# q, k and v by Strassen's scheme in a two-layer attention kernel, with shared activation sums and an earlier bias of q

## The chip, the cores and the metric

The kernel runs on one NeuronCore of a Trainium2 chip. The metric is the device time of one execution in microseconds (us), as a median over runs. Engines are called as in the profile: PE is TensorE (matmuls), PEld its weight loads, DVE is VectorE, ACT is ScalarE, POOL is GpSimd, SP is SyncE, which only starts DMAs here.

## The reference, cut to what matters

Two attention layers are computed on `x` of 8 images x 512 channels x 32 x 32 positions (1024 tokens), all in float32. Only the first layer's opening is touched by the change:

```python
h = group_norm(xf, gn_w, gn_b)                       # 8 x 512 x 1024
qkv = jnp.einsum('oc,bct->bot', qkv_w, h) + qkv_b[None, :, None]
q, k, v = jnp.split(qkv, 3, axis=1)                  # 8 heads of 64 channels
q = fake_quant(q)                                    # scale from min and max of the whole tensor
k = fake_quant(k)
v = fake_quant(v)
```

After it come softmax attention per head, a projection with the residual, and the second layer (norm, one-head attention over 512 channels, projection, residual). Because `fake_quant` takes its scale from the minimum and maximum over all images, q, k and v of all images have to be there before the first attention score.

## The kernel before, in words

The work has two stages. Stage 1 computes q, k and v of all images, stores them in DRAM and gathers their extremes. Stage 2 first turns the extremes into scales and then runs attention, projection and the whole second layer, with the matmuls of several images woven into one another by a planner (`attention`, `fold`, `others`, lines 438 to 756). `mm` (line 93) ties every matmul to the one before it, so TensorE runs them exactly in the order in which the program makes them; one matmul that waits holds all that follow. The other engines' queues are static too; their order is laid down when the program is built, and an instruction that needs nothing may be put ahead of one that stands earlier in the text.

In stage 1 an image `b` (0 to 7) has its 512 channels on 128 partitions as 4 chunks `cc`, and its 1024 tokens as two halves `hf` of 512. `load_x` (line 231) loads it on SP's queue. `norm_steps` (line 100) is a generator: statistics of each chunk and half on VectorE (lines 107 and 108), a small matmul with `gavg` that averages over the channels of a group (line 111), four small VectorE operations, a second small matmul (line 121), the power on GpSimd (line 124), and 8 scalings into `h` (line 128). The loop calls it as `ahead` for image b+1 while image b is multiplied, one step at a time.

q and k of an image are 8 tiles `t` of 128 channels (0 to 3 are q, 4 to 7 are k; `j` is t modulo 4). Each takes 8 matmuls of 512 columns into a pair of PSUM banks (`pair_ps`, two pairs in all). VectorE then adds the bias, writes the tile to SBUF and takes the maximum in one instruction (line 321), takes the minimum in a second (line 325), and SP stores the tile (line 326). v of an image is 8 tiles of 128 tokens, each of 4 matmuls into one bank (`bank`, two in all), then an add of the bias, a maximum, a minimum and a store (lines 343 to 346).

Image 0 is opened by hand: its norm is cut into the 4 chunks, and the matmuls of its first two tiles (`early`) go chunk by chunk as the norm gets ready. `bias` (line 264) multiplies the weights with the norm's shift: 4 matmuls of 512 columns, then for q and k `by_channel` (line 213: four multiplications by the identity, line 216, and a reduction, line 217) and an add. For q it stands after the opening's last matmul. The weights that stage 2 folds into one another (`wn`: NQ1 and NK1 in tile `h`, NV1 and WP1 in tile `v`) are loaded on SP's queue at b = 1. The pool `l1p` has one buffer for each tag (`h`, `v`, `g`, `rs`, `rs1`, `acc1`), which stage 2 uses too.

At the end of stage 1, lines 351 to 374 reduce the extremes over all partitions, VectorE quantises the first pair, and TensorE meanwhile runs the first half of `fold` (line 674): 16 matmuls on `wn_h` before the first scores, then 16 on `wn_v` between the next scores.

Of the kernel before, what the change touches and what calls it, by code (L numbers as in the profile page):

```python
# [9 lines left out]
F32 = mybir.dt.float32  # L10
# [36 lines left out]
def attn_pair_kernel(  # L47
# [51 lines left out]

    def norm_steps(src, dst, wcol, bank, nm, ccs=range(CC)):  # L100

# [3 lines left out]
        for i, cc in enumerate(ccs):  # L105
            for hf in range(NH):
                nc.vector.bn_stats(st[:, i, hf, :], src(cc, hf))
            nc.vector.bn_aggr(mv[:, i, :], st[:, i, :, :].rearrange("p a s -> p (a s)"))
        yield
        ps = bank(f"gps_{nm}")[:, 0:n]  # L110
# [15 lines left out]
        for hf in range(NH):  # L126
            for i, cc in enumerate(ccs):
# [3 lines left out]
                )  # L131
        yield

# [19 lines left out]
    with ExitStack() as fast:  # L153
# [5 lines left out]
        def pair_ps(name):  # L159
            return ps_s.tile([P, 2, 512], F32, tag="s", name=name)  # L160
# [4 lines left out]
        def bank(name):  # L165
            return ps_o.tile([P, 512], F32, tag="o", name=name)
# [11 lines left out]

        qmax = wts.tile([P, B * PAIRS], F32, name="qmax")
        qmin = wts.tile([P, B * PAIRS], F32, name="qmin")  # L180
        kmax = wts.tile([P, B * PAIRS], F32, name="kmax")
        kmin = wts.tile([P, B * PAIRS], F32, name="kmin")
        vmax = wts.tile([P, B * NT], F32, name="vmax")
        vmin = wts.tile([P, B * NT], F32, name="vmin")

# [4 lines left out]
        NR0, NR1 = B * PAIRS * 16, B * NH * 4  # L190
        rcs = l1p.tile([P, NR0 + NR1], F32, name="rcs")
        rs_d = [dram.tile([4, 512], F32, tag=f"rs{n}", name=f"rs_d{n}") for n in range(B * PAIRS)]
        rs1_d = [dram.tile([4, P], F32, tag=f"rs1{n}", name=f"rs1_d{n}") for n in range(B * NH)]
# [24 lines left out]

        with tc.tile_pool(name="p1w", bufs=1) as p1w, tc.tile_pool(name="p1", bufs=2) as p1, tc.tile_pool(
            name="p1o", bufs=4  # L220
        ) as p1o:
            wqkv = p1w.tile([P, CC, 3 * C], F32, name="wqkv")

            wn = {}
            for tag, ij in (("h", (NQ1, NK1)), ("v", (NV1, WP1))):
                two = l1p.tile([P, 2, CC, C], F32, tag=tag, name=f"wn_{tag}")
                for n, i in enumerate(ij):
                    wn[i] = two[:, n]
            xs, hs = {}, {}

# [6 lines left out]

            def norm(b, parts=1):

                xt = xs.pop(b)  # L240
                hs[b] = hn = p1.tile([P, CC, T], F32, tag="h", name=f"h1_{b}")
                n = CC // parts
                return [
                    norm_steps(
                        lambda cc, hf: xt[:, cc, bass.ts(hf, 512)],
                        lambda cc, hf: hn[:, cc, bass.ts(hf, 512)],
                        V_GN0W, av_bank, f"a{b}_{i}", range(i * n, (i + 1) * n),
                    )
                    for i in range(parts)
                ]  # L250

            load_x(0)
            for i in (1, 2):
                nc.sync.dma_start(
                    wqkv[:, :, bass.ts(i, C)], w_qkv[:, :, bass.ts(i, C)]
                )
            vb = p1w.tile([P, C], F32, name="vb")
            nc.scalar.dma_start(vb, vbias[0:1, :].partition_broadcast(P))
            load_x(1)
            gbb = p1w.tile([P, CC, P], F32, name="gbb")  # L260
            widen(gbb, V_GN0B)
            qkb = p1w.tile([P, 2 * PAIRS], F32, name="qkb")

            def bias(i):

                ps = bank(f"bias{i}")
                for _ in weigh(ps, ((wqkv[:, :, bass.ts(i, C)], gbb),)):
                    pass
                if i == 2:
                    nc.vector.tensor_add(vb, vb, ps)  # L270
                    return
                b4 = qkb[:, bass.ts(i, PAIRS)]
                by_channel(b4, ps)
                nc.vector.tensor_add(
                    b4, b4, vec[:, V_QKB + i * PAIRS : V_QKB + (i + 1) * PAIRS]
                )
# [14 lines left out]
            for cc in range(CC):  # L291
                for t in range(2):
                    for hf in range(NH):
                        qk_mm(0, early[t], t, hf, cc)
                        if (cc, hf) in ((0, 1), (1, 0), (1, 1)):
                            next(next(then, iter(())), None)
            for b in range(B):
                ahead = norm(b + 1)[0] if b + 1 < B else iter(())
                next(ahead, None)
                if b + 2 < B:  # L300
                    load_x(b + 2)
                if b == 1:
                    nc.sync.dma_start(wp0, w_sq[WP0])
                    for i, w in wn.items():
                        nc.sync.dma_start(w, w_sq[i])
                hn = hs[b]
                for t in range(2 * PAIRS):
                    isk, j = divmod(t, PAIRS)
                    g = b * PAIRS + j
                    if b == 0 and t < 2:  # L310
                        ps = early[t]
                    else:
                        ps = pair_ps(f"qkps_{b}_{t}")
                        for hf in range(NH):
                            for cc in range(CC):
                                qk_mm(b, ps, t, hf, cc)
                    if b == 0 and j == 0:
                        bias(isk)
                    qk = p1o.tile([P, T], F32, tag="qk", name=f"qk1_{b}_{t}")
                    mx, mn = (kmax, kmin) if isk else (qmax, qmin)  # L320
                    nc.vector.tensor_scalar(  # L321
                        qk, ps.rearrange("p a n -> p (a n)"), qkb[:, t : t + 1], None,
                        ALU.add, ALU.max, accum_out=mx[:, g : g + 1],
                    )
                    nc.vector.tensor_reduce(mn[:, g : g + 1], qk, AX.X, ALU.min)
                    nc.sync.dma_start((k_d if isk else q_d)[b][j], qk)
                    if t in (3, 5, 6):
                        next(ahead, None)
                for t in range(NT):
                    g = b * NT + t  # L330
                    ps = bank(f"vps_{b}_{t}")
                    for cc in range(CC):
                        mm(
                            ps,
                            lhsT=hn[:, cc, bass.ts(t, P)],
                            rhs=wqkv[:, cc, 2 * C : 3 * C],
                            start=(cc == 0),
                            stop=(cc == CC - 1),
                        )
                    if b == 0 and t == 0:  # L340
                        bias(2)
                    vt = p1o.tile([P, C], F32, tag="v", name=f"v1_{b}_{t}")
                    nc.vector.tensor_add(vt, ps, vb)
                    nc.vector.tensor_reduce(vmax[:, g : g + 1], vt, AX.X, ALU.max)
                    nc.vector.tensor_reduce(vmin[:, g : g + 1], vt, AX.X, ALU.min)
                    nc.sync.dma_start(v_d[b][:, t, :], vt)
                del hs[b]

# [769 lines left out]
```

## Time and profile before

| what | value |
|---|---|
| median of 3 runs | 2965.43 us (2964.5 to 2966.43) |
| the profiled execution's own time | 2966.03 us |
| its span, first to last instruction | 2964.5 us |
| mean granted clock of TensorE | 0.998 of full |
| TensorE busy | 2932.2 us, 8772 instructions |
| VectorE busy | 1442.7 us |
| ScalarE busy | 718.6 us |
| first q and k matmul of image 0 starts | 14.0 us |
| last matmul of stage 1 ends | 700.57 us |

A row of a group reads: line, engine, operation, tile written, tiles read, shapes, count, then the busy time in us and the mean of one in ns, then the idle time of the engine just before and what ended it. In the chain, pieces stand in order of time with start and length. `x` counts instructions. All matmuls stand under line 94, the helper `mm`, so the tile's name tells which they are: `qkps` is q and k, `vps` is v, `gps_a` the norm's small ones. Rows on one engine may overlap by some tens of ns.

### The profile page before, as it was taken

The numbers are of one execution on the slowest core, as the hardware profiler recorded it, in microseconds if no ns is written. First come the engines' busy times: TensorE is split into PE (matmuls) and PEld (weight loads), VectorE is DVE, ScalarE is ACT, GpSimd is POOL, SyncE is SP. The second block draws the span as 40 slices with busy tenths as digits, with TensorE's granted clock in tenths as the row PEclk, the third lists the DMA queues.
The fourth block names the chain that finished last, engine by engine and source line by source line (L and its number), as shares of the span: only waits on it lengthen the run. The fifth ranks groups of instructions, "written<-read, shape, count | busy, mean of one in ns | idle before, by whom it ended". The sixth has DMA issues, their size and how long they took to land.

```text
span 2964.5 us, 22733 instructions
## 1 busy us (share of the span) xinstructions
PE 2932.2 (99%) x8772; PEld 1170.9 (39%) x8772; DVE 1442.7 (49%) x1980; ACT 718.6 (24%) x825; POOL 26.1 (1%) x28
## 2 busy tenths in 40 slices
PE   7999999999999999999999999999999999999999
PEld 3444444443233333333333333334333333333443
DVE  5555554446874446345544544463446444543311
ACT  0000000002642333233233233332333332332001
POOL 0000000000000000000000000000000000000000
PEclk9999999999999999999999999999999999999999
DMA  6322221123220111012011211110211021000000
GB/s 244 114 107 102 107 107 75 71 78 128 79 65 29 61 50 54 15 61 73 31 44 48 67 36 58 40 54 29 61 54 50 23 67 61 15 26 29 18 14 23
DMA packets 112518, 182.81 MB, mean 62 GB/s; under 512 B 22032, under 2 KB 54800, under 8 KB 111760
## 3 DMA queue, kind: packets, MB, share of 16 engines
q1 hardware_dynamic: 112112, 180.98, 18.1%
q8 instruction: 70, 1.15, 0.2%
q10 hardware_dynamic: 288, 0.29, 0.1%
q14 instruction: 48, 0.39, 0.0%
HBM read 113.53 MB, written 67.40 MB: 61 GB/s over the span
## 4 chain that ended last, share of the span: by engine, by line
PE 95%; DVE 2%; DMA 1%; issue 1%; SPq 0%; POOL 0%; ACT 0%; DVEq 0%; POOLq 0%; ACTq 0%
PE o L94 15%; PE s L94 15%; PE qkps L94 15%; PE av L94 14%; PE g L94 8%; PE v2ps L94 7%; PE pj L94 7%; PE vps L94 7%; PE st L94 4%; DVE acc L464 1%; PE sm L94 1%; PE fold L94 1%; DMA rs<-rs_d 0%; PE bias L94 0%; DMA raw<-k_d 0%
## 5 line engine op out<-in xcount | busy, mean ns | idle before, releaser
L459 ACT ACTIVATE pt<-st,esc 128x1024 f32<-128x1024 f32 x512 | 542.3, 1112 | 665.6 <-PE st L94 664.2
L464 DVE TENSOR_TENSOR acc<-acc,pt 128x1024 f32<-128x1024 f32 x384 | 469.9, 1224 | 208.1 <-ACT pt L459 192.6
L94 PE MATMUL av<-pt,v 128*64 128x512 f32 x2048 | 476.6, 601 | 0.0
L94 PE MATMUL qkps<-h,wqkv 128*128 128x512 f32 x1024 | 449.5, 598 | 8.8 <-DVE qk L321 6.6
L94 PE MATMUL o<-p,v 128*128 128x512 f32 x1024 | 452.1, 596 | 1.5 <-DVE x L663 1.5
L94 PE MATMUL s<-g,h 128*128 128x512 f32 x1024 | 450.3, 596 | 0.0
L94 PEld LDWEIGHTS qkps<-h,wqkv 128*128 128x128 f32 x1024 | 194.3, 192 | 246.4 <-issue 240.9
L94 PEld LDWEIGHTS s<-g,h 128*128 128x128 f32 x1024 | 191.7, 190 | 243.4 <-issue 242.6
L94 PEld LDWEIGHTS o<-p,v 128*128 128x128 f32 x1024 | 191.5, 190 | 241.6 <-issue 240.0
L94 PEld LDWEIGHTS av<-pt,v 128*64 128x64 f32 x2048 | 132.2, 136 | 260.9 <-issue 260.9
L94 PE MATMUL pj<-ao,wp 128*128 128x512 f32 x512 | 226.0, 597 | 2.4 <-DVE ao L501 2.4
L94 PE MATMUL g<-h,wa 128*128 128x512 f32 x512 | 224.9, 595 | 0.0
L94 PE MATMUL v2ps<-wm,h 128*128 128x512 f32 x512 | 222.9, 594 | 0.0
L94 PE MATMUL vps<-wqkv,h 128*128 128x512 f32 x512 | 221.3, 592 | 0.8 <-DVE vb L270 0.8
L321 DVE TENSOR_SCALAR_CACHE_REDUCE qk<-qkps,qkb 128x1024 f32<-128x1024 f32 x64 | 82.1, 1283 | 222.7 <-PE qkps L94 222.6
L685 ACT COPY wa<-fold 128x512 f32<-128x512 f32 x4 | 2.3, 586 | 709.2 <-PE fold L94 709.2
L631 ACT ACTIVATE p<-s 128x512 f32<-128x512 f32 x128 | 76.4, 597 | 364.0 <-PE s L94 364.0
L635 DVE TENSOR_TENSOR acc<-acc,p 128x512 f32<-128x512 f32 x96 | 66.4, 692 | 186.4 <-ACT p L631 186.4
L94 PE MATMUL st<-q,k 64*128 64x512 bf16 x1024 | 156.5, 382 | 0.0
L462 DVE TENSOR_TENSOR acc<-pt,pt 128x1024 f32<-128x1024 f32 x64 | 78.3, 1224 | 140.0 <-ACT pt L459 140.0
L94 PEld LDWEIGHTS vps<-wqkv,h 128*128 128x128 f32 x512 | 97.2, 190 | 123.6 <-issue 122.0
L94 PEld LDWEIGHTS pj<-ao,wp 128*128 128x128 f32 x512 | 96.0, 190 | 124.8 <-issue 119.4
(118 smaller groups left out, 1315.1 us busy)
## 6 DMA issues: line engine op xcount, KB each, us to landing
x<-in_x_dram SPq DMA_DIRECT2D x32, 512.0 KB
q_d<-qk SPq DMA_DIRECT2D x32, 512.0 KB
raw<-q_d SPq DMA_DIRECT2D x32, 512.0 KB
k_d<-qk SPq DMA_DIRECT2D x32, 512.0 KB
raw<-k_d SPq DMA_DIRECT2D x32, 512.0 KB
v_d<-v SPq DMA_DIRECT2D x64, 256.0 KB
raw<-v_d SPq DMA_DIRECT2D x32, 512.0 KB
x<-in_x_dram SPq DMA_DIRECT2D x64, 256.0 KB
```

What stands on the lines that cost most here:

```text
L94: ins = nc.tensor.matmul(*args, **kw).ins
L321: nc.vector.tensor_scalar(qk, ps.rearrange("p a n -> p (a n)"), qkb[:, t : t + 1], None, ALU.add, ALU.max, accum_out=mx[:, g : g + 1],)
L459: nc.scalar.activation(pt, st, AF.Exp, scale=esc)
L462: nc.vector.tensor_add(accs[b, j, hf], pts[u - 1], pt)
L464: nc.vector.tensor_add(accs[b, j, hf], accs[b, j, hf], pt)
L631: nc.scalar.activation(pt, ps, AF.Exp, scale=SM1)
L635: nc.vector.tensor_add(acc, acc, pt)
L685: nc.scalar.copy(dst[:, e, :], ps)
```

## The change

For images b = 1 to 7 the products are made by Strassen's scheme with 7 products of half-size blocks instead of 8. For q and k the left matrix is (q weights; k weights) by (channel half `K0`, channel half `K1`), and the right one is (channel halves) by (token halves). One `qk_block` makes the 128 channels `j` of q and of k together: 7 products of 2 matmuls with 512 columns. For v the weights' two halves of 256 columns take the place of the token halves on the other side; one `v_block` makes 4 tiles of tokens at once: 7 products, each of 4 matmuls with 256 columns. The sums of activations (`token_sums`, four per image, written once into the buffers `h` and `v` in turn) serve both; the sums of weights (`weight_sums`) are made once, during the v loop of image 0, in the space of `wa`, `wm` and `g`.

Each block uses two banks, `x` and `y`. Partial results that several outputs share are copied out while the bank goes on adding: by ScalarE with the bias (`keep`) for q and k, by VectorE for v. The last additions are fused with the maximum in one VectorE instruction (`add_max`). `TURNS` gives the order in which the products of two `qk_block`s (0 and 1) and one `v_block` (2) are made, 21 for one half of an image, and after every second one a step of `ahead`, which is now cut finer (13 steps with the sums, of which one or two instructions on most; `fine`).

Besides: the norm is written in place and the images have three buffers instead of two; image 0 is multiplied as before, with the steps of image 1's norm and sums and the sums of weights spread over it; the bias of q is made after the third chunk of the opening, ahead of its last one, and that of k and v at the first k and v tile; `vb` is held twice; the extremes lie in the tile `rcs`; and the folded weights are loaded on ScalarE's queue, `h` at b = 7 and `v` after the last image.

```diff
-    def norm_steps(src, dst, wcol, bank, nm, ccs=range(CC)):
+    def norm_steps(src, dst, wcol, bank, nm, ccs=range(CC), fine=False):
...
+            if fine and i + 1 < n:
+                yield
...
-        yield
+                if fine and i % 2 == 1:
+                    yield
+        if not fine:
+            yield
...
+        N_MAX = PAIRS * (1 + (B - 1) * NH)
+        cut, at = {}, 0
+        for name, n in (
+            ("qmax", N_MAX), ("kmax", N_MAX), ("vmax", NT * B), ("qmin", B * PAIRS),
+            ("kmin", B * PAIRS), ("vmin", NT + (B - 1) * NT // 2),
+        ):
+            cut[name] = rcs[:, at : at + n]
+            at += n
+        qmax, kmax, vmax, qmin, kmin, vmin = cut.values()
...
-        with tc.tile_pool(name="p1w", bufs=1) as p1w, tc.tile_pool(name="p1", bufs=2) as p1, tc.tile_pool(
+        with tc.tile_pool(name="p1w", bufs=1) as p1w, tc.tile_pool(name="p1", bufs=3) as p1, tc.tile_pool(
...
+            def load_folded(tag, ij):
                 two = l1p.tile([P, 2, CC, C], F32, tag=tag, name=f"wn_{tag}")
                 for n, i in enumerate(ij):
                     wn[i] = two[:, n]
-            xs, hs = {}, {}
+                    nc.scalar.dma_start(wn[i], w_sq[i])
...
+                hs[b] = xt = xs.pop(b)
...
+            K0, K1 = slice(0, CC // 2), slice(CC // 2, CC)
+            ss = []
+            vs = l1p.tile([P, 4, CC // 2, C // 2], F32, tag="g", name="vs")
+            def weight_sums():
+                tt = nc.vector.tensor_tensor
+                for half in (wa, wm):
+                    ss.extend(half[:, i : i + 2, :] for i in (0, 2))
+                (a11, a12), (a21, a22) = (
+                    [wqkv[:, k, bass.ts(i, C)] for k in (K0, K1)] for i in (0, 1)
+                )
+                tt(ss[0], a21, a22, ALU.add)
+                yield
+                tt(ss[1], ss[0], a11, ALU.subtract)
+                yield
+                tt(ss[2], a11, a21, ALU.subtract)
+                yield
+                tt(ss[3], a12, ss[1], ALU.subtract)
+                yield
+                (w11, w12), (w21, w22) = (
+                    [wqkv[:, k, 2 * C + i * C // 2 : 2 * C + (i + 1) * C // 2] for i in (0, 1)]
+                    for k in (K0, K1)
+                )
+                tt(vs[:, 0], w11, w12, ALU.subtract)
+                yield
+                tt(vs[:, 1], w22, vs[:, 0], ALU.subtract)
+                yield
+                tt(vs[:, 2], w22, w12, ALU.add)
+                yield
+                tt(vs[:, 3], w21, vs[:, 1], ALU.subtract)
+                yield
+            def quarters(b):
+                h = hs[b]
+                return [h[:, k, bass.ts(hf, 512)] for k in (K0, K1) for hf in range(NH)]
+            def token_sums(b):
+                a, b_, c, d = quarters(b)
+                cs[b] = t = l1p.tile(
+                    [P, 4, CC // 2, 512], F32, tag="hv"[b % 2], name=f"sums_{b}"
+                )
+                tt = nc.vector.tensor_tensor
+                tt(t[:, 0], b_, a, ALU.subtract)
+                yield
+                tt(t[:, 1], d, t[:, 0], ALU.subtract)
+                yield
+                tt(t[:, 2], d, b_, ALU.subtract)
+                yield
+                tt(t[:, 3], c, t[:, 1], ALU.subtract)
+                yield
+            def prepare(b, bank):
+                yield from norm(b, bank=bank, fine=True)[0]
+                yield from token_sums(b)
+            def add_max(dst, ps, other, mx):
+                nc.vector.tensor_tensor_reduce(
+                    dst, ps, other, 1.0, -3.0e38, ALU.add, ALU.max, accum_out=mx
+                )
+            def qk_block(b, j):
+                a, _, c, d = quarters(b)
+                t1, t2, t3, t4 = (cs[b][:, i] for i in range(4))
+                a11, a12, a22 = wqkv[:, K0, 0:C], wqkv[:, K1, 0:C], wqkv[:, K1, C : 2 * C]
+                s1, s2, s3, s4 = ss
+                ps = pair_ps(f"qkps_{b}_{j}")
+                x, y = ps[:, 0, :], ps[:, 1, :]
+                u = p1o.tile([P, 2, 512], F32, tag="u", bufs=2, name=f"u_{b}_{j}")
+                u4 = p1o.tile([P, 512], F32, tag="u4", bufs=1, name=f"u4_{b}_{j}")
+                q = p1o.tile([P, T], F32, tag="qk", name=f"q1_{b}_{j}")
+                k = p1o.tile([P, T], F32, tag="qk", name=f"k1_{b}_{j}")
+                bq, bk = qkb[:, j : j + 1], qkb[:, PAIRS + j : PAIRS + j + 1]
+                def product(ps, w, r, start):
+                    for i in range(CC // 2):
+                        mm(
+                            ps, lhsT=w[:, i, bass.ts(j, P)], rhs=r[:, i, :],
+                            start=start and i == 0, stop=(i == CC // 2 - 1), skip_group_check=True,
+                        )
+                def keep(dst, bias):
+                    nc.scalar.activation(dst, x, AF.Identity, bias=bias)
+                def store(t, mn, dst):
+                    nc.vector.tensor_reduce(
+                        mn[:, b * PAIRS + j : b * PAIRS + j + 1], t, AX.X, ALU.min
+                    )
+                    nc.sync.dma_start(dst[b][j], t)
+                product(x, a11, a, True)
+                keep(u[:, 0, :], bq)
+                yield
+                product(y, a12, c, True)
+                add_max(q[:, 0:512], y, u[:, 0, :], column("qmax", qmax))
+                yield
+                product(x, s2, t2, False)
+                keep(u[:, 1, :], bk)
+                yield
+                product(y, s3, t3, True)
+                yield
+                product(x, s1, t1, False)
+                keep(u4, bk)
+                add_max(k[:, 512:T], y, u4, column("kmax", kmax))
+                yield
+                product(x, s4, d, False)
+                nc.vector.tensor_scalar(
+                    q[:, 512:T], x, bq, None, ALU.add, ALU.max, accum_out=column("qmax", qmax)
+                )
+                store(q, qmin, q_d)
+                yield
+                product(y, a22, t4, False)
+                add_max(k[:, 0:512], y, u[:, 1, :], column("kmax", kmax))
+                store(k, kmin, k_d)
+                yield
+            def v_block(b, n):
+                a, _, c, d = quarters(b)
+                t1, t2, t3, t4 = (cs[b][:, i] for i in range(4))
+                lo, hi = slice(2 * C, 2 * C + C // 2), slice(2 * C + C // 2, 3 * C)
+                w11, w21, w22 = wqkv[:, K0, lo], wqkv[:, K1, lo], wqkv[:, K1, hi]
+                s1, s2, s3, s4 = (vs[:, i] for i in range(4))
+                x, y = (av_bank(f"vps_{b}_{n}_{i}").rearrange("p (t c) -> p t c", t=2)
+                        for i in range(2))
+                u = l1p.tile([P, 2, 2, C // 2], F32, tag="rs", name=f"uv_{b}_{n}")
+                u4 = l1p.tile([P, 2, C // 2], F32, tag="rs1", name=f"uv4_{b}_{n}")
+                v = [p1o.tile([P, 2, C], F32, tag="v2", bufs=3, name=f"v1_{b}_{n}_{i}")
+                     for i in range(2)]
+                vlo, vhi = vb[:, :, 0 : C // 2], vb[:, :, C // 2 : C]
...
+                product(x, a, w11, True)
+                nc.vector.tensor_add(u[:, 0], x, vlo)
+                yield
+                product(y, c, w21, True)
+                add_max(v[0][:, :, 0 : C // 2], y, u[:, 0], column("vmax", vmax))
+                yield
+                product(x, t2, s2, False)
+                nc.vector.tensor_add(u[:, 1], x, vlo)
+                yield
+                product(y, t1, s3, True)
+                yield
+                product(x, t3, s1, False)
+                nc.vector.tensor_add(u4, x, vhi)
+                add_max(v[1][:, :, C // 2 : C], y, u4, column("vmax", vmax))
+                yield
+                product(x, t4, w22, False)
+                add_max(v[0][:, :, C // 2 : C], x, vhi, column("vmax", vmax))
+                store(0)
+                yield
+                product(y, d, s4, False)
+                add_max(v[1][:, :, 0 : C // 2], y, u[:, 1], column("vmax", vmax))
+                store(1)
+                yield
...
+            vb = p1w.tile([P, 2, C], F32, name="vb")
+            for i in range(2):
+                nc.scalar.dma_start(vb[:, i, :], vbias[0:1, :].partition_broadcast(P))
...
+                if cc == 2:
+                    bias(0)
+            load_x(2)
+            ahead = prepare(1, av_bank)
+            more = weight_sums()
+            hn = hs[0]
...
+                if t == PAIRS:
+                    bias(1)
...
+                if t > 0:
+                    next(ahead, None)
...
                 next(ahead, None)
+                next(more, None)
+            for rest in (ahead, more):
+                for _ in rest:
+                    pass
+            TURNS = (0, 0, 2, 0, 0, 2, 0, 2, 0, 0, 2, 1, 1, 2, 1, 1, 2, 1, 2, 1, 1)
+            for b in range(1, B):
                 if b + 2 < B:
                     load_x(b + 2)
                 if b == 1:
                     nc.sync.dma_start(wp0, w_sq[WP0])
+                if b == B - 1:
+                    load_folded("h", (NQ1, NK1))
+                ahead = prepare(b + 1, bank) if b + 1 < B else iter(())
+                for n in range(2):
+                    blocks = (qk_block(b, 2 * n), qk_block(b, 2 * n + 1), v_block(b, n))
+                    for i, turn in enumerate(TURNS):
+                        next(blocks[turn])
+                        if i % 2 == 1:
+                            next(ahead, None)
+                for _ in ahead:
+                    pass
+                del hs[b], cs[b]
+            load_folded("v", (NV1, WP1))
```

## The prediction, made before the changed kernel was run

> **What bounds the kernel now.** I read the page's first two parts first, then the chain of work that ended last.
>
> ```profile
> PE 2932.2 (99%) x8772; PEld 1170.9 (39%) x8772; DVE 1442.7 (49%) x1980; ACT 718.6 (24%) x825; POOL 26.1 (1%) x28
> ...
> PE   7999999999999999999999999999999999999999
> ...
> DVE  5555554446874446345544544463446444543311
> ACT  0000000002642333233233233332333332332001
> ...
> PE 95%; DVE 2%; DMA 1%; issue 1%; SPq 0%; POOL 0%; ACT 0%; DVEq 0%; POOLq 0%; ACTq 0%
> ```
>
> TensorE is busy 99% of the span and 95% of the chain: time goes down only where it gets less work or waits less. The stage that changes is the first nine and a half slices, where VectorE is about half busy and ScalarE does nothing.
>
> Next I read that chain in order of time for the stage (start, length, what; x counts instructions):
>
> ```profile
> 121.25 27.47 PE qkps L94 x64
> 148.84 13.84 PE qkps L94 x32
> 162.80 13.84 PE qkps L94 x32
> 176.63 27.47 PE vps L94 x64
> 204.10 27.46 PE qkps L94 x64
> ```
>
> One image repeats every 204.10 - 121.25 = 82.85 us with nothing but matmuls in it. The program's 96 matmuls of an image stand there as 192 instructions, two each, so one instruction takes 27.47 / 64 = 0.4292 us and a matmul of 512 columns 0.858 us; the 0.45 left over are the four small ones of the norm. The stage ends at 700.57, when the first fold matmul starts.
>
> The one long hole of TensorE in the stage is in the timeline of the start:
>
> ```profile
> 31.95 3.60 PE L94 MATMUL bias<-wqkv,gbb 128*128 128x512 f32 x8
> ...
> 35.59 0.30 DVE L216 TENSOR_TENSOR bias<-bias,ident 128x128 f32<-128x128 f32 x1 [2.24 <-PE bias L94]
> 35.79 0.68 DVE L107 BATCH_NORM_STATS2 gst_a<-x 128x6 f32<-128x512 f32 x1
> ...
> 40.77 1.27 DVE L321 TENSOR_SCALAR_CACHE_REDUCE qk<-qkps,qkb 128x1024 f32<-128x1024 f32 x1
> ...
> 42.19 4.19 PE L94 MATMUL qkps<-h,wqkv 128*128 128x512 f32 x5 [6.64 <-DVE qk L321]
> ```
>
> The bias of q is the last matmul of the opening; VectorE turns it into a column between statistics of a later image, and only then frees the first PSUM pair. TensorE stands 6.64 us.
>
> VectorE's prices, from the groups by shape within the first 360 us:
>
> ```profile
> L321 DVE TENSOR_SCALAR_CACHE_REDUCE qk<-qkps,qkb 128x1024 f32<-128x1024 f32 x32 | 41.0, 1283 | 97.3 <-PE qkps L94 97.3
> L107 DVE BATCH_NORM_STATS2 gst_a<-x 128x6 f32<-128x512 f32 x56 | 36.2, 674 | 2.3 <-DMA x<-in_x_dram 2.3
> L343 DVE TENSOR_TENSOR v<-vps,vb 128x512 f32<-128x512 f32 x29 | 20.0, 690 | 31.8 <-PE vps L94 31.7
> L325 DVE TENSOR_REDUCE kmin<-qk 128x1 f32<-128x1024 f32 x16 | 19.5, 1216 | 0.3
> L128 DVE TENSOR_SCALAR h<-x,gmean_a,grstd_a 128x512 f32<-128x512 f32 x40 | 19.0, 543 | 0.3
> ```
>
> [...] The trace has 429 ns for 512 fp32 columns, and no 256-column matmul. [...] The trace lists 190 ns a load, and one load starts with each matmul, every 0.43 us, with 0.24 us idle between loads. [...] `ao<-ao,scl,rs` with two fp32 SBUF sources of 1024 takes 1282 ns[...].
>
> **The change part by part.**
>
> *Matmuls of b = 1 to 7.* q and k: 7 products of 2 matmuls instead of 16, for each of 4 j: 56 for 64. v: 14 products of 4 half-wide matmuls, which are 28 full ones, for 32. So 12 x 0.858 = 10.30 us less per image, all on TensorE and on the path: 7 x 10.30 = **-72.1 us**. An image becomes 72.1 us plus 0.45 for the norm.
>
> *Width of v's matmuls.* 784 instructions (14 x 4 x 2 x 7) have 256 columns, each with its own load of 128 columns. I price one at half of 429, 215 ns. Below that there is no reason to go. From above: the load's 190 ns still fits under 215, so it is hidden; if 25 ns of it were not, +20 us; if none of it, 784 x 0.19 = +149 us. I take 0.
>
> *ScalarE.* 12 copies with bias per image; the row of the same kind, `g<-g,gb` 128x512, is 687 ns: 8.2 us on an idle engine. The tightest: the sixth product of a q/k block adds onto the half bank that ScalarE copied after the fifth; one product of v, 4 x 0.4292 = 1.72 us, lies between. Hidden, 1 us to spare; uncovered it would be 0.7 us for each of 28 blocks.
>
> *VectorE.* The fused add-and-max from PSUM is in no row. Lower bound 0.69 (the plain add)[...]; I take 0.69 + 0.08 for reading out the maximum, a DVE_READ_ACCUMULATOR row of L321 = 0.78. [...] Per image: 20 fused 15.6, 4 of these 3.3, 12 minima of 1024 at 1.22 14.6, 6 adds 4.1, the norm as before 11.5 (8 x 0.67 + 4 x 0.21 + 8 x 0.54 + small), 4 token sums at 1.22 (a tensor_tensor of 1024, row L464) 4.9: 54 us of 72.5, 75%; before it was about 48 of 83. Unevenly: `ahead` gets 10 of its 13 steps in the first half of an image, so that half holds 18.8 + 13.8 = 32.6 us of 36.1, the second 22.5.
>
> Walking the 21 turns of a first half at 1.72 us: TensorE overwrites a bank two turns or more after VectorE could take it, except behind ScalarE's copy. The seventh product of a q/k block waits for copy 0.69 + fused 0.78 out of 3.43 us, so VectorE may be 1.8 us behind there. After turn 10 it has two evictions and two minima queued and clears them about 20.0 us into the half; the norm's second small matmul stands after turn 12, at 20.7 us, and needs four more operations of 0.15. That is level: this added wait holds all of TensorE's queue. I take 1 us for each of six images with an `ahead`, **+6**[...].
>
> *b = 0.* Its q, k, v stay. In its v loop VectorE gets 2.05 a tile plus a norm or sum step (1.1 to 1.2) plus a weight sum (1.22 or 0.69): with the second `vb` add 32.6 us against TensorE's 27.5 + 3.4. The backlog peaks near 3 us, about what two PSUM banks absorb: **+1**, bounds 0 and 6.
>
> *Bias of q moved.* Its 8 instructions now stand before the last chunk's 8 (4 matmuls), so they end 3.43 us before the opening does, not with it. VectorE's six operations (4 x 0.29 + 0.68 + 0.15 = 2.0) and the first pair's eviction (1.28) just fit under that chunk if no statistics stand among them; before, 4.3 us of them did (six L107, two aggregates), and if the same ones stand there again, the stall is 6.64 - 3.43 = 3.2. So it shrinks by 3.4 to 6.6: **-5**. It passes nothing on SP or POOL.
>
> *Loads.* The folded weights' 4 x 1 MB leave SP near the start and go to ScalarE's queue: two at b = 7, behind the sums of b = 6, with ScalarE's first copy queued behind two issues of about 0.45 us; that copy has 3.4 us: 0. Two after the last product. Their first reader stood 14.4 us after the stage's end (fold of wn_v at 714.94), covered by 13.7 us of fold matmuls on wn_h. At the 342 GB/s seen in 710 to 715, 2 MB take 6 us, and DMA was 16% busy in 700 to 705: 0, at worst +6. The third x buffer lets x(2) start earlier, after x(1); nothing waits for it. The second `vb` copy (256 KB): 0.
>
> Sum against the profiled execution: span 2964.5 - 72.1 - 5 + 6 + 1 = 2894.4; its own time, 2966.0, is 1.5 more: 2895.9. The median, 2965.4, lies 0.6 below that execution, so **2895**.
>
> **The rivals.** *VectorE's order and backlog hold TensorE* (0.20): its queue is static, and the trace shows statistics of later images put between urgent work (35.79 above). For it: 90% load in first halves. Against: in b = 1 to 7 of before nothing urgent was late. At 4 us for six images and 6 for b = 0, 30 instead of 7: 2918. *Half-wide matmuls carry a fixed cost* (0.10): 25 ns on each of 784 gives 2915. *No stall at all* (0.05): 2964.5 - 72.1 - 6.6 + 0.9 = 2887. *Slower: weight loads come out from under the half-wide matmuls* (0.07): each load then follows the matmul before it; 2895 + 149 = 3044. It decides from 70 / 784 = 90 ns an instruction. For it: loads would fill 190 of 215 ns. Against: around the norm's pair of 4-column matmuls at 75.2 us three loads of 128 columns start 0.11 us apart, so loads can follow each other far faster than 215 ns.
>
> **How the numbers follow.** Forecast 0.58, the others as given. The range goes from 2886 (no stall) to 2925 (both middle rivals, with a late wn_v load); what is left out is the slow rival and a heavier fixed cost, some 0.12. Faster by over 0.2% (5.9 us, about what a measurement of this kernel can tell from no change) 0.91, within 0.02 (the far tail of the fixed cost), slower 0.07.
>
> **What would show it.** Image period 73 to 74 us; vps instructions at 215 ns pitch; fused operations near 0.78; the hole before the third qkps pair at 3 us or less; TensorE waiting for `gd_a` or the bank readers under 2 us an image; no wait of fold on wn_v. A period above 77, or a vps pitch above 240, would make the prediction wrong.

## The result, and the profile after

The changed kernel takes **2993.23 us** (median of 4 runs, 2992.26 to 2995.55) against 2965.85 for the kernel before in runs on the same chip: ratio 1.0094, 95% interval 1.0077 to 1.0112. It is 0.9% slower, where 2895 us, 2.4% faster, was predicted. The span of the profiled execution is 2991.8 us, 27.3 more than before, at the same granted clock (0.998).

The page of the changed kernel, first two parts and the shares of the chain:

```profile
PE 2889.8 (97%) x8996; PEld 1205.5 (40%) x8996; DVE 1478.8 (49%) x2143; ACT 776.5 (26%) x909; POOL 26.6 (1%) x28
...
PE   7988888889999999999999999999999999999999
...
DVE  6655565534785446444634454464446344543311
ACT  0010000011653333233333233332333232332001
...
PE 90%; DVE 5%; DMA 2%; ACT 1%; issue 1%; SPq 0%; DVEq 0%; POOL 0%; ACTq 0%
```

TensorE does have less to do: 2889.8 us of busy time where it had 2932.2. But the seven slices that lie wholly in images 1 to 7 have gone from 9 to 8, and 5% of the chain that ended last are on VectorE, 2% before. Neither VectorE nor ScalarE is anywhere near full in those slices.

Stage 1 ends at 725.4 us instead of 700.57, so 24.8 of the 27.3 us are in it. Cut at the same marks, before and after: the third pair of the opening starts at 42.51 instead of 42.19 (+0.3); image 0 ends at 122.10 instead of 121.25 (+0.5 on top of that); images 1 to 7 take 603.3 instead of 579.3 (**+24.0**, where -66 was forecast); and 2.5 us are lost after the stage. So the miss is about 90 us in images 1 to 7, or 90 / 28 = 3.2 us for each block of q and k. Their period, from the chain of the changed kernel in order of time (start, length, what):

```profile
163.77 3.71 PE qkps L94 x8
...
206.57 3.71 PE qkps L94 x8
...
250.04 3.71 PE qkps L94 x8
```

The same place recurs once in each half of an image: 250.04 - 163.77 = 86.3 us for an image, where 73 to 74 was expected and 82.85 stood before.

What TensorE waits for in images 1 to 7, from the waits of the changed kernel between 120 and 726 us (us in total, times, longest):

```profile
PEld qkps L94 <- ACT u L353: 84.8, 56, 1.6
...
PEld qkps L94 <- DVE q L377: 47.6, 28, 1.8
...
PE qkps L94 <- ACT u L353: 42.9, 56, 0.8
...
PE qkps L94 <- DVE q L377: 24.4, 28, 1.0
```

The counts are the finding: 56 is twice 28 and 28 is once 28. Each block of q and k waits twice for a ScalarE copy and once for VectorE's plain eviction, with the same regularity in every image. A backlog of VectorE would hardly spread so evenly; the third experiment tests it. (A wait is listed twice, at the weight load and at the matmul; the two are not added.) The timeline of the changed kernel shows two of the three in one half of image 3:

```profile
300.86 1.88 PE L94 MATMUL qkps<-sums,wa 128*128 128x512 f32 x4
302.78 0.69 ACT L353 ACTIVATE u<-qkps,qkb 128x512 f32<-128x512 f32 x1 [5.52 <-PE qkps L94]
303.52 1.98 PE L94 MATMUL qkps<-sums,wm 128*128 128x512 f32 x4 [0.78 <-ACT u L353]
...
310.52 1.98 PE L94 MATMUL qkps<-x,wm 128*128 128x512 f32 x4
312.54 0.75 DVE L377 TENSOR_SCALAR_CACHE_REDUCE q<-qkps,qkb 128x512 f32<-128x512 f32 x1 [1.14 <-PE qkps L94]
313.36 1.98 PE L94 MATMUL qkps<-sums,wqkv 128*128 128x512 f32 x4 [0.85 <-DVE q L377]
```

At 300.86 TensorE makes the third product, into bank `x`; ScalarE copies `x` at 302.78; and the fourth product, at 303.52, starts only when that copy is done. But the fourth product writes bank `y`, and what the second had left there was evicted by 300.2 us (at 299.43 in the same timeline, 0.69 long and 0.08 for reading out the maximum). The same happens at 313.36: the seventh product, into `y`, waits for the eviction of `x` after the sixth. From start to start these products take 2.66 and 2.84 us, where four instructions take 1.72. `x` and `y` are two halves of **one tile** (`pair_ps`), so the suspicion is that the wait goes by the tile.

### The profile page after: what moved, and what is told of

Same layout as the page of the kernel before. It is cut to its first block, busy times and chain, and to the rows that moved or that the text cites. A ratio compares the mean times of both kernels' runs of the same rounds, so it can differ in the third digit from the quotient of the medians.

```text
span 2991.8 us, 23419 instructions
## 1 busy us (share of the span) xinstructions
PE 2889.8 (97%) x8996; PEld 1205.5 (40%) x8996; DVE 1478.8 (49%) x2143; ACT 776.5 (26%) x909; POOL 26.6 (1%) x28
## 4 chain that ended last, share of the span: by engine, by line
PE 90%; DVE 5%; DMA 2%; ACT 1%; issue 1%; SPq 0%; DVEq 0%; POOL 0%; ACTq 0%
PE s L94 15%; PE o L94 14%; PE av L94 13%; PE qkps L94 13%; PE g L94 7%; PE v2ps L94 7%; PE pj L94 7%; PE vps L94 6%; PE st L94 4%; DVE acc L672 1%; ACT u L353 1%; PE sm L94 1%; DVE q L377 1%; DVE rcs L411 1%; DMA rs<-rs_d 1%
## 5 line engine op out<-in xcount | busy, mean ns | idle before, releaser
L94 PE MATMUL av<-pt,v 128*64 128x512 f32 x2048 | 476.3, 600 | 0.0
L94 PE MATMUL o<-p,v 128*128 128x512 f32 x1024 | 452.1, 596 | 1.5 <-DVE x L871 1.5
L94 PE MATMUL s<-g,h 128*128 128x512 f32 x1024 | 450.3, 596 | 0.0
L94 PEld LDWEIGHTS s<-g,h 128*128 128x128 f32 x1024 | 191.7, 190 | 243.4 <-issue 242.6
L94 PEld LDWEIGHTS o<-p,v 128*128 128x128 f32 x1024 | 191.5, 190 | 241.6 <-issue 239.8
L94 PEld LDWEIGHTS av<-pt,v 128*64 128x64 f32 x2048 | 132.1, 136 | 260.0 <-issue 260.0
L94 PE MATMUL pj<-ao,wp 128*128 128x512 f32 x512 | 225.2, 596 | 2.7 <-DVE ao L709 2.5
L94 PE MATMUL g<-h,wa 128*128 128x512 f32 x512 | 224.9, 595 | 0.0
L94 PE MATMUL v2ps<-wm,h 128*128 128x512 f32 x512 | 222.9, 593 | 0.0
L353 ACT ACTIVATE u<-qkps,qkb 128x512 f32<-128x512 f32 x84 | 57.7, 687 | 620.1 <-PE qkps L94 620.1
L94 PE MATMUL qkps<-x,wqkv 128*128 128x512 f32 x352 | 171.8, 622 | 25.2 <-ACT u L353 21.1
L94 PE MATMUL st<-q,k 64*128 64x512 bf16 x1024 | 156.6, 381 | 2.4 <-ACT pt L667 2.2
L94 PEld LDWEIGHTS pj<-ao,wp 128*128 128x128 f32 x512 | 95.9, 190 | 125.4 <-issue 119.2
L94 PEld LDWEIGHTS g<-h,wa 128*128 128x128 f32 x512 | 96.0, 190 | 124.5 <-issue 115.0
L94 PEld LDWEIGHTS v2ps<-wm,h 128*128 128x128 f32 x512 | 96.7, 190 | 122.1 <-issue 122.1
L827 DVE COPY v<-v2ps 128x512 f32<-128x512 f32 x64 | 44.2, 691 | 202.6 <-PE v2ps L94 202.6
L815 ACT ACTIVATE g<-g,gb 128x512 f32<-128x512 f32 x64 | 44.0, 687 | 317.3 <-PE g L94 317.3
```

Of the source, the lines that this page charges most:

```text
L94: ins = nc.tensor.matmul(*args, **kw).ins
L353: nc.scalar.activation(dst, x, AF.Identity, bias=bias)
L815: nc.scalar.activation(g[:, oc, :], ps, AF.Identity, bias=gb[:, oc : oc + 1])
L827: nc.vector.tensor_copy(vt[:, t, :], ps)
```

## The experiments

**The theory**: in the built program a product waits for the reader of the product before it wherever both lie in the same tile, though in different banks. `TURNS` puts three such pairs of a block next to each other (products 1 and 2, 3 and 4, 6 and 7), at about 1 us each. **The rivals**: VectorE is too late with its queue (the rival of the prediction); the v part does not pay; the miss comes from the opening.

**Two tiles instead of one.** The two banks of a block become two tiles of one bank each, in a pool of four banks again; image 0 and stage 2 keep pairs (the lines that open and close the pools are left out here).

```diff
...
-                ps = pair_ps(f"qkps_{b}_{j}")
-                x, y = ps[:, 0, :], ps[:, 1, :]
+                x, y = (scope["q"].tile([P, 512], F32, tag=f"q{i}", name=f"qkps_{b}_{j}_{i}")
+                        for i in range(2))
...
```

> Theory (pair wait): in the changed kernel x and y of a q/k block are two banks of one PSUM tile, and each product waits for the reader of the product before it, though that reader is in the other bank. With x and y as two tiles of one bank each the three adjacent products of a block no longer wait: an image goes from 86.3 to 73 to 74 us, 7 images give about -88, so about 2905 us. Rival (VectorE late): TensorE waits because VectorE's queue is behind; its work is the same here, so the time stays at 2993 within 0.3%.

Measured: 2901.81 us (2900.55 to 2902.34), ratio to the kernel before 0.9785 (0.9769 to 0.9802), 91.4 us below the changed kernel. The chain of this kernel now has one recurring piece an image:

```profile
156.83 5.42 PE qkps L94 x12
...
229.94 5.42 PE qkps L94 x12
...
303.04 5.42 PE qkps L94 x12
```

The period is 73.1 us. Its timeline at the same place of a block, third and fourth product:

```profile
273.04 1.88 PE L94 MATMUL qkps<-sums,wa 128*128 128x512 f32 x4
274.76 1.88 PE L94 MATMUL qkps<-sums,wm 128*128 128x512 f32 x4
274.96 0.69 ACT L353 ACTIVATE u<-qkps,qkb 128x512 f32<-128x512 f32 x1 [4.47 <-PE qkps L94]
276.47 1.89 PE L94 MATMUL vps<-wqkv,x 128*128 128x256 f32 x8
```

The fourth product starts 1.72 us after the third and runs beside the copy. Where the 91 us had stood shows in the busy times of images 1 to 7, first of the changed kernel, then of this one (window, its length, then PE, PEld, DVE, ACT and POOL busy with their instructions, granted clock, DMA share, GB/s):

```profile
120.00:722.00 602.00, 534.58 (x1592) 291.60 (x1591) 325.85 (x630) 57.71 (x84) 6.04 (x6) 1.00 0.25 94
```

```profile
120.00:630.00 510.00, 509.11 (x1592) 300.17 (x1591) 319.61 (x628) 57.71 (x84) 6.04 (x6) 1.00 0.29 111
```

The same 1592 instructions take 602 us there and 510 here. Of the 92, 67 were idle (602 - 534.58), and 25 were booked as busy. The listed times are why: in an unbroken row a product is listed with 1.88 us, but the next one follows after 1.72 and covers the rest; at a wait nothing covers it, and the product behind is listed with 1.98. That is some 0.27 us at each of 84 waits. With two tiles TensorE is busy 509 of 510 us, and VectorE has all but the same work (319.61 us for 325.85).

**Only the order of the products.** The tile stays; another block's product is put between the two of each pair.

```diff
-            TURNS = (0, 0, 2, 0, 0, 2, 0, 2, 0, 0, 2, 1, 1, 2, 1, 1, 2, 1, 2, 1, 1)
+            TURNS = (0, 2, 0, 1, 0, 2, 0, 1, 0, 2, 0, 1, 0, 2, 1, 2, 1, 2, 1, 2, 1)
```

> Only the order of the products changes, none of a q/k block follows another of the same block directly; x and y stay one tile. Pair wait: one product of 1.72 us then lies between, enough for ScalarE's copy (0.69) and nearly enough for copy and fused add (1.47): about 2905 to 2920 us. VectorE late: same work for VectorE, evictions bunched more at the end of a half: 2993 or more.

Measured: 2913.29 us (2912.47 to 2917.4), ratio 0.9828 (0.9812 to 0.9845), 80 below the changed kernel. So it is neighbourhood within one tile that costs, not the tile as such. The other 11.5 us stay because VectorE's reading sometimes comes later than one product. From this kernel's waits:

```profile
PE qkps L94 <- DVE q L377: 5.8, 6, 1.0
...
PE qkps L94 <- DVE rcs L327: 2.5, 7, 0.4
```

The plain eviction of q now holds TensorE six times instead of 28, once in each image that prepares the next one, and the fused one seven times. With 1.0 us for v (line 427) that is 9.3 us. In this order VectorE does come late, though by little.

**A lighter VectorE.** In the changed kernel the minima of images 1 to 7 read 8 elements instead of 1024.

```diff
-                        mn[:, b * PAIRS + j : b * PAIRS + j + 1], t, AX.X, ALU.min
+                        mn[:, b * PAIRS + j : b * PAIRS + j + 1], t[:, 0:8], AX.X, ALU.min
...
-                    nc.vector.tensor_reduce(column("vmin", vmin), v[i], AX.XY, ALU.min)
+                    nc.vector.tensor_reduce(column("vmin", vmin), v[i][:, :, 0:4], AX.XY, ALU.min)
```

> The changed kernel, whose minima of images b >= 1 read 8 elements a row instead of 1024 (so a part of the minima is left out, and the scales may be others): VectorE gets some 12 us less work an image. Pair wait: the three waits of a q/k block are for ScalarE's copy and for the fused or plain eviction itself, not for a queue, so little changes: 2985 to 2993. VectorE late: most of the 90 us go, 2900 to 2930.

Measured: 2993.04 us (2991.51 to 2994.21), ratio 1.0096 (1.0079 to 1.0113), the changed kernel's own time. The window of images 1 to 7, and below it the wait of this kernel:

```profile
120.00:722.00 602.00, 534.15 (x1591) 291.24 (x1590) 244.32 (x649) 57.74 (x84) 6.05 (x6) 1.00 0.25 94
```

```profile
PE qkps L94 <- ACT u L353: 42.9, 56, 0.8
```

82 us of VectorE's work are gone (325.85 to 244.32) and nothing moves. That refutes the rival of a late VectorE for images 1 to 7 of the changed kernel.

**v alone, three tries.** q and k in the old way, v by `v_block`, first with its seven products back to back:

```diff
...
+                    for t in (2 * n, 2 * n + 1, PAIRS + 2 * n, PAIRS + 2 * n + 1):
...
+                        next(ahead, None)
+                    for _ in range(7):
+                        next(blocks[2])
+                        next(ahead, None)
```

> q and k of images b = 1 to 7 as in the kernel before, only v by Strassen (x and y of a v block are separate tiles anyway). Pair wait: v's part pays in full, 4 x 0.858 x 7 = -24 us against the kernel before, plus some 3.5 us of opening and stage end as in the changed kernel: about 2945. Rival (half-wide matmuls or VectorE's v work cost what they save): 2966 or more.

Measured: 2982.25 us (2981.27 to 2983.16), ratio 1.0056 (1.0039 to 1.0073). Missed: back to back, v's products outrun VectorE, which reads all but one of them and has a step of `ahead` besides (`PE vps L94 <- DVE uv L428`: 18.4 us in 14 waits; 5.2 more go to the norm's second small matmul). That placement is not the change's, so the run says nothing on v in it. Next, v's products woven between the halves of the q and k tiles:

```diff
+                            if hf == 0 or i < 3:
+                                next(blocks[2])
...
-                    for _ in range(7):
-                        next(blocks[2])
                         next(ahead, None)
```

> v alone by Strassen again, but its seven products are woven between half tiles of q and k (8 matmuls apart in time, 3.43 us), and the norm's steps stand after q and k tiles. Theory: in the first form of this run v's products stood back to back with a step of the norm after each, and waited for VectorE (up to 2.0 us); woven, v's part pays in full: -24 us and some 3.5 for opening and stage end, about 2945. Rival (half-wide matmuls cost what they save): 2966 or more.

Measured: 2969.71 us (2967.66 to 2973.18), ratio 1.0014 (1.0005 to 1.0022). Missed again, but its last image, which has no `ahead`, takes 39.56 us a half: the products were in place and the norm's steps were not. Two of them in a row bring the two small matmuls of the norm together, and the second holds TensorE's queue for 3 us, 17.9 in six images (the timeline is in the last section). With one step after the first half of each tile and one after the tile:

```diff
+                            if hf == 0:
+                                next(ahead, None)
...
-                        next(ahead, None)
                         next(ahead, None)
```

> v alone by Strassen, woven between half tiles of q and k, with the norm's steps no longer two in a row: in the run before, the norm's second small matmul stood right behind the first one and TensorE waited 3 us for VectorE there. Theory: an image takes 79.5 us, all of v's saving: about 2945. Rival (half-wide matmuls cost what they save): 2966 or more.

Measured: 2942.54 us (2940.77 to 2945.06), ratio 0.9925 (0.9909 to 0.9942), 22.5 us below the kernel before. v needs 28 matmuls for 32 in 7 images: 28 x 0.858 = 24.0 us to be gained. So v's part pays, half-wide matmuls and all; between 400 and 640 us the chain of this kernel has matmuls of TensorE and nothing else.

**The opening held.** The statistics of images 1 to 7 and the weight sums are ordered behind the first eviction of q (in the diff, `pin` adds that dependency).

```diff
...
-                nc.vector.bn_stats(st[:, i, hf, :], src(cc, hf))
+                pin(nc.vector.bn_stats(st[:, i, hf, :], src(cc, hf)))
...
-                tt = nc.vector.tensor_tensor
+                tt = lambda *a: pin(nc.vector.tensor_tensor(*a))
...
```

> The changed kernel with VectorE's statistics of images b >= 1 and the sums of weights held behind the first q eviction. Theory: these were put into the opening's chain (2.1 us before the last chunk, 3.1 us before the third pair); held back, both close: about 2988 us, 0.15% less than the changed kernel. Rival: the opening waits for its loads, and nothing is gained: 2993.

Measured: 2985.51 us (2984.05 to 2987.14), ratio 1.0068 (1.0051 to 1.0085), 7.7 below the changed kernel. First the third pair in the timeline of the changed kernel, then in this one's:

```profile
42.51 17.84 PE L94 MATMUL qkps<-x,wqkv 128*128 128x512 f32 x37 [3.14 <-DVE qk L505]
```

```profile
36.45 20.87 PE L100 MATMUL qkps<-x,wqkv 128*128 128x512 f32 x48 [0.32 <-DVE qk L511]
```

It starts 6.1 us earlier. What stood in the way is in the changed kernel's timeline of VectorE:

```profile
23.48 1.21 DVE L282 TENSOR_TENSOR wa<-wqkv 128x1024 f32<-128x1024 f32 x1
...
24.68 1.22 DVE L286 TENSOR_TENSOR wm<-wqkv 128x1024 f32<-128x1024 f32 x1
25.82 0.15 DVE L121 TENSOR_TENSOR gd_a<-gd_a,gmv_a 128x1 f32<-128x1 f32 x1
...
37.91 0.68 DVE L298 TENSOR_TENSOR vs<-wqkv 128x512 f32<-128x512 f32 x1
```

The weight sums stand in the v loop of image 0 in the program's text, but they need only the weights, and the static order puts them into the opening. The first two stand between the norm's small operations, so that the last of these, `gd_a`, comes at 25.82; the third stands, with others, between the multiplications of the bias. TensorE waits for both. The first wait, in the changed kernel and below it before the change:

```profile
26.03 0.51 PE L94 MATMUL gps_a<-gd_a,gavg 128*128 128x1 f32 x2 [2.60 <-DVE gd_a L121]
26.41 6.09 PE L94 MATMUL qkps<-x,wqkv 128*128 128x512 f32 x10
```

```profile
23.90 0.38 PE L94 MATMUL gps_a<-gd_a,gavg 128*128 128x1 f32 x2 [0.51 <-DVE gd_a L118]
```

The wait costs more than its length. The ten matmul instructions behind it are listed with 6.09 us, at a granted clock of 0.52 between 26 and 29 us and 0.91 between 29 and 32. With the hold the same ten take

```profile
24.73 4.54 PE L100 MATMUL qkps<-x,wqkv 128*128 128x512 f32 x10
```

That is 4.37 us to the start of the next row (29.10), where the changed kernel has 5.93 (26.41 to 32.34). Behind the 3.14 us at 42.51 the clock is 0.65 between 42 and 46 us; with the hold that wait is 0.32 us, and the 48 instructions behind it take 20.70 us to the next row (57.15), for 22.40 in the changed kernel (42.51 to 64.91). So of the 7.7 us 6.1 are there when the third pair starts, and the rest comes behind it.

**Both repairs, and the late load.** The two tiles and the held opening together:

> Two single-bank tiles and the held VectorE work together. If both theories hold and don't overlap: 2901.8 - 7.5 = 2894. If the hold only moves work into the first Strassen images, where VectorE is three quarters busy, it gives part of that back: 2897 to 2902.

Measured: 2894.64 us (2893.74 to 2895.27), ratio 0.9756 (0.9743 to 0.9769), 7.2 below the kernel of two tiles alone. Then this kernel without the load of `wn_v` after the last product; its fold reads the other pair's weights, so this one leaves a part out and only bounds the cost:

```diff
-            load_folded("v", (NV1, WP1))
+            wn[NV1], wn[WP1] = wn[NQ1], wn[NK1]
```

> As the run with two tiles and the hold, without the load of NV1 and WP1 (their fold reads the other pair's weights, so the second layer's values are others). It bounds what the late load costs: 2 to 3 us less if it is the cause of the waits 25 us after the stage's end, no change if those come from elsewhere.

Measured: 2890.21 us (2889.34 to 2890.92), ratio 0.9741 (0.9727 to 0.9754): the load costs 4.4 us, more than the 2 to 3 expected. Last, the load stays and goes to SP's queue:

```diff
-                    nc.scalar.dma_start(wn[i], w_sq[i])
+                    (nc.sync if tag == "v" else nc.scalar).dma_start(wn[i], w_sq[i])
```

> As the run with two tiles and the hold, but the last folded weights (NV1, WP1) are issued on SP's queue, so that one of their two loads stands behind the last store of k. Theory: at the stage's end the 2 MB hold up that store, and with it x's and the second pair's loads and then TensorE for some 2 us; about 1 to 2 us less. Rival: the order of issue doesn't matter[...]: no change.

Measured: 2890.66 us (2888.29 to 2892.69), ratio **0.9743** (0.9729 to 0.9756), 75.2 us faster than the kernel before and 102.6 than the changed one. It keeps the whole computation. How the load delays in the changed kernel is in its chain and timelines at the stage's end:

```profile
726.33 8.59 DMA k_d<-k
```

```profile
735.26 3.66 SPq L751 DMA_DIRECT2D x<-in_x_dram  x8
```

The last store of k takes 8.6 us to land with 2 MB of `wn_v` issued just before it. The `x` loads of stage 2 stand behind that store on SP: they leave 9.9 us after the stage's end, and left 4.8 us after it before the change:

```profile
705.41 3.65 SPq L543 DMA_DIRECT2D x<-in_x_dram  x8
```

The second pair's `raw` is behind them: VectorE starts to quantise it at 746.75, after 12.03 us of waiting for it, and comes late to the sums of ScalarE's results; ScalarE waits for those sums (1.13 us at 754.21, 0.69 at 756.01), and TensorE for ScalarE:

```profile
757.18 0.39 PE L94 MATMUL st<-q,k 64*128 64x512 bf16 x2 [1.41 <-ACT pt L667]
```

With both repairs and the load on SP's queue the `x` loads leave 7.9 us after the stage's end (631.56 for 623.70). In the kernel of two tiles alone, with the load on ScalarE's queue, TensorE waits for ScalarE 30 to 31 us after the stage's end (0.19 and 0.94 us); with the load on SP's it has no such wait in the first 46 us after it. Why two microseconds on the `x` loads are enough to win back 4.0 of the 4.4 was not followed further.

## Why the prediction was wrong, step by step

*What bounds the kernel: right.* With the waits gone the stage is TensorE's alone (509 of 510 us).

*Matmuls, -72.1: right.* The image period of 73.1 with two tiles and the 22.5 us of v alone confirm the count and the 0.858.

*Width of v's matmuls, 0: right.* In the changed kernel eight instructions take 1.73 us from start to start:

```profile
305.34 1.89 PE L94 MATMUL vps<-wqkv,x 128*128 128x256 f32 x8
307.07 1.88 PE L94 MATMUL qkps<-sums,wa 128*128 128x512 f32 x4
```

That is 216 ns each at 256 columns, and 429 at 512. The 215 priced was the author's estimate, half of 429; no row of the kernel before showed it. Of the rivals, the fixed cost of half width and the slower one by weight loads are out.

*The VectorE step failed*, in this sentence: "TensorE overwrites a bank two turns or more after VectorE could take it, except behind ScalarE's copy." It walked the turns bank by bank. The program waits by tile, so the second product of each pair waits for a reader of the first, which it has nothing to do with and which only starts when the first is done. The exception named, the sixth product, has a product of v for cover: in the groups by shape of the changed kernel TensorE has 0.0 us of idle time before its row, `qkps<-x,wm`. The three pairs without cover were not looked at. ScalarE's copies, "hidden, 1 us to spare", were hidden only where that product of v stands; the term was put at 0, and is two thirds of the waits. The size is 91.4 us by experiment, 3.3 for each block. The prices in that step were right: the same groups have the fused operation and the q eviction as

```profile
L327 DVE CUSTOM_DVE_ANT_0 k<-qkps,u 128x512 f32<-128x512 f32 x53 | 36.7, 692 | 50.3 <-ACT u L353 28.9 <-PE qkps L94 21.4
...
L377 DVE TENSOR_SCALAR_CACHE_REDUCE q<-qkps,qkb 128x512 f32<-128x512 f32 x26 | 19.4, 747 | 14.7 <-PE qkps L94 14.7
```

With 0.083 for reading out the maximum that is 0.775 and 0.83; the prediction had 0.78, and 3.3 for four q evictions. The stall of 6 us that the walk arrived at did not come: with two tiles less than 1 us of idle time is left in all seven images. The rival's 4 us an image was the author's estimate, and no run showed it. The walk added listed times up, to 54 us an image and some 360 for the seven; neighbouring rows overlap, and VectorE was busy 319.6 us there.

*b = 0, +1: right* (+0.5 beyond the later start of the opening's end). *Bias of q moved, -5: wrong*, the third pair starts 0.3 us later instead. The hole in front of it did shrink, from 6.64 to 3.14 us, about the smaller gain that the step had named, with statistics still in between. What the step had at nothing is the 2.60 us of waiting at 26.03, where 0.51 stood before, and the slow matmuls behind it: the weight sums, which were counted in the v loop of image 0 alone, stand there. The rival's reason, the static order of VectorE, was right for the opening. With the order held the third pair starts at 36.45, 5.7 us earlier than before the change: that is the -5. The hold itself is worth 7.7 us in the changed kernel and 7.2 with two tiles.

*Loads, 0 and at worst +6: inside the bounds, by another way.* The first reader of `wn_v` was indeed covered, and that was the only one looked at. The cost comes, as far as the traces show, through a store and the transfers of stage 2 that stand behind it on SP.

The sum, by the marks of the first section: the span grew by 27.3 us where it was to shrink by 70.1, so 97.4 us were missed. 5.3 of them are in the opening (+0.3 for -5), -0.5 in the rest of image 0 (+0.5 for +1), 90.1 in images 1 to 7 (+24.0 for -66.1) and 2.5 behind the stage (for 0). By experiment the pair's waits are worth 91.4, the order in the opening 7.2 and the late load 4.4. The last two were measured in the kernel of two tiles; the changed kernel itself loses only 2.5 behind the stage, so the load's share is smaller in it.

The slower case came true, at 0.07, but not by its mechanism. What was missing among the rivals is a wait between two neighbours that share only a name.

## What to carry to other kernels

Count a wait on PSUM by the tile that the program tracks, not by the bank (here 91.4 us): an accumulator that is read while another runs gets a tile of its own, or other work between (80 us here). Walk each pair of neighbours on the bounding engine, not only the loads of the others: here ScalarE, busy 57.71 of 602 us, and VectorE, busy 325.85, held TensorE in every block, and counts of a wait that are whole multiples of the blocks (56 and 28 for 28 blocks) point to that. Work that was ready early, the weight sums, went where the static order had room, in the opening; a hold there was worth 7.7 us, so an urgent stretch needs an order of its own.

## What the runs showed of the hardware that was not expected

ScalarE read one bank of a block while TensorE wrote the other, and neither got slower: with two tiles the copy at 274.96 takes 0.69 us, and the product beside it 1.71 to the start of the next (274.76 to 276.47), as elsewhere.

In the first woven run of v a hole of 3 us in TensorE was followed by slow matmuls in some images and not in others. The hole in one image, then the eight instructions behind it in three images, from the chain (start, length, what), then the window after the third of these holes, with the granted clock third from the end:

```profile
323.92 0.39 PE L94 MATMUL gps_a<-gd_a,gavg 128*128 128x4 f32 x2 [2.99 <-DVE gd_a L121]
```

```profile
156.12 6.32 PE qkps L94 x8
...
241.61 3.54 PE qkps L94 x8
...
324.31 5.24 PE qkps L94 x8
```

```profile
324.00:330.00 6.00, 6.00 (x13) 2.93 (x14) 4.50 (x11) 0.00 (x0) 1.01 (x1) 0.72 0.07 26
```

Eight matmul instructions take 3.43 us elsewhere. Six images have the hole, 17.9 us in all and none over 3.0, and the eight behind it take 6.32, 3.54, 5.24, 6.22, 3.54 and 5.24 us in turn; in the six us behind the third the granted clock is 0.72. So the same hole cost between nothing and almost 3 us more than itself, 9.5 us in the six. With the 17.9 us of the holes that is the 27 us between this run and the next. What decides between the cases no run here shows.

Shorter holes did it too: behind the 2.60 us in the opening of the changed kernel the clock was 0.52, and in the run of v back to back, where the third image has a hole of 2.02 us before v's sixth product, the sixteen instructions from that product on take 5.41, 3.74, 5.41, 3.73, 5.41 and 3.73 us in the six images. The waits of the changed kernel in images 1 to 7, 0.8 us and often, left it at 1.00.
